# A fused adaLN block: the order of its opening, the loads and the third weight group

## The chip, the cores and the metric

The kernel runs on one core of one Trainium2 chip. The metric is device time in microseconds (us). The engines of the core are called by the names of the profile: PE is TensorE (matrix products), DVE is VectorE, ACT is ScalarE, POOL is GpSimd, and SP is SyncE, which here only issues DMAs.

## The reference, cut to what matters

```python
mod = (silu(c) @ wmod).reshape(2, 6, 1, 512)      # sa, ca, ga, sb, cb, gb
h = layernorm(x) * (1 + ca) + sa                  # x: 2 x 4096 x 512, float32
xn = h / norm(h) * sqrt(512) * gamma
q, kv, a = split(xn @ W_qkva.T, 3)                # W_qkva: 1536 x 512
y = scan(y[t] = sigmoid(a[t]) * y[t-1] + kv[t])   # along the 4096 tokens
x = x + floor(ga) * (q * y)
h = layernorm(x) * (1 + cb) + sb
x = x + floor(gb) * fp4_ffn(h)                    # gate, up, down: 512 -> 1408 -> 512
```

`floor` keeps the sign and raises the magnitude to at least 0.25. `fp4_ffn` quantises activations and weights to FP4 in blocks of 16. The change lies wholly in the first half, ahead of the first scans.

## The kernel before

The 8192 tokens are cut into 64 tiles of 128 tokens, and into 16 blocks of 512. The first half runs 64 **slots**: slot `4*i + e` multiplies block `i` by group `e` of the q/kv/a weights (group `e` holds 128 output features of each of the three parts, taken in the order `PARTS = (2, 1, 0)`). A product is float16 in two pieces: each operand is split into a high part (rounded to float16) and a low part (the rest), and three of the four combinations are summed, so one slot is 36 matmuls of 128x512 (`mix`, L393). Slot 0 is cut into four quarters of 128 tokens, so it can begin when the first tile is there.

To get an input tile ready, the kernel loads it (`norm_load`), takes its moments on DVE (`norm_moments`, L153), the inverse deviation on POOL (`norm_stats`, L160 and L161), centres and scales (`norm_center`, L166), shifts (`norm_shift`, L172), squares on ACT (`norm_square`, L354), computes the gain by a power on POOL (`norm_gain`, L359 and L361), writes the high part on ACT (`norm_hi`, L367) and the low part on DVE (`norm_lo`, L372), and transposes both by a DMA from SP (L376).

A weight group is prepared in a similar way: three loads (`load_part`, L208), a product with gamma (`gamma_qkva`, L281, on POOL unless DVE is asked for), squares on ACT (`square_qkva`, L285), a power on POOL (`inverse_qkva`, L288 and L289), the high part on ACT or DVE (`hi_qkva`, L308 or L310), the low part on DVE (`lo_qkva`, L316) and a transposing DMA (L324). `gain_qkva` (L296, L299) computes the factor with which the gate is scaled.

High and low parts share four buffers (`new_hl`). The modulation rows are products on PE (`mod_spread`, `mod_rows`, `mod_columns`) that use two PSUM buffers of their own; `mod_store` (L262, L263) copies such a row on ACT and sends it to DRAM from POOL. The products of a slot use PSUM banks 0 to 2 or 3 to 5 in turn. They are read in the next slot by `gates` (ACT, L405), `scan` (DVE, L411) and `read_out` (DVE, L420), and with these reads the banks come free for the slot after.

The order of work on every engine is written out by hand: all five engines issue their instructions in the order of the program, and the function `start` (L642 and the lines after it) is the opening, ahead of slot 0. SP works through its DMAs in program order too, and waits at each until its source is ready. Slots follow in a loop: input tile `slot + 4` gets its high and low parts, tile `slot + 5` is centred, shifted and squared, tile `slot + 6` gets its moments.

In the kernel before, groups 0 and 1 are prepared in `start`; group 2 is multiplied and squared in slot 0 and split in slot 1; group 3 is multiplied and squared in slot 1 and split in slot 2.

Of the kernel before, what the change touches and what calls it, by code (L numbers as in the profile page):

```python
# [17 lines left out]
P = 128  # L18
D = 512
KC = D // P  # L20
# [23 lines left out]
def tile_adaln_block(  # L44
# [147 lines left out]
    wm = {}  # L192
# [14 lines left out]
    def load_part(e, part):  # L207
        S.dma_start(wq[e, part], w_qkva[part * D + e * P : part * D + (e + 1) * P, :])  # L208

    def load_mod(s, pieces=1):  # L210
        w = KC // pieces
        for k in range(0, KC, w):
            S.dma_start(
                wm[s][:, k : k + w, :],
                wmod[k * P : (k + w) * P, s * D : (s + 1) * D].rearrange("(k p) e -> p k e", p=P),
            )
# [63 lines left out]
    def gamma_qkva(e, part, engine=G):  # L280
        engine.tensor_tensor(wq[e, part], wq[e, part], gam, ALU.mult)  # L281
# [5 lines left out]
    def inverse_qkva(e, a=0, b=3):  # L287
        V.tensor_scalar(rs[:, e, a:b], us[:, e, a:b], 1e-36, 2.0**-28, ALU.max, ALU.mult)  # L288
        G.tensor_tensor(rs[:, e, a:b], rs[:, e, a:b], mhalf[:, : b - a], ALU.pow)  # L289
# [40 lines left out]
    def norm_load(g):  # L330
        i, t = divmod(g, KC)
        if i not in xrows:
            xrows[i] = apool.tile([P, KC, D], F32, name="xr", tag="xr", bufs=4)
        xld[g] = xrows[i][:, t, :]
        b, t0 = divmod(g * P, N)
        S.dma_start(xld[g], x[b, t0 : t0 + P, :])

    def norm_moments(g):
        xstat[g] = moments(xld[g])

    def norm_stats(g):
        xstat[g] = mean_rstd(xstat[g])

    def norm_center(g):
        xh[g] = center(xld.pop(g), xstat[g][0], ca[g * P // N])
# [294 lines left out]
    sa = [ctile([P, D], F32, "sa0", tag="mod_s0"), None]  # L640

    def start():  # L642
        load_mod(1, KC)
        norm_load(0)
        load_mod(0, 2)
        S.dma_start(gam, gamma.partition_broadcast(P))
        for part in PARTS:
            load_part(0, part)
        for g in range(1, KC):
            norm_load(g)  # L650
        for part in PARTS:
            load_part(1, part)
        load_mod(2)
        pc = mod_spread(1, 0)
        ps = mod_spread(0, 0)
        r1 = mod_rows(1)
        r0 = mod_rows(0)

        norm_moments(0)
        norm_stats(0)  # L660
        A.activation(ca[0], pc, AF.Copy, bias=1.0)
        a, b_, c_ = PARTS
        gamma_qkva(0, a, V)
        square_qkva(0, a)
        gamma_qkva(0, b_, V)
        square_qkva(0, b_)
        inverse_qkva(0, a, a + 1)
        gamma_qkva(0, c_, V)
        inverse_qkva(0, b_, b_ + 1)
        norm_center(0)  # L670
        hi_qkva(0, a, True)
        square_qkva(0, c_)
        norm_moments(1)
        hi_qkva(0, b_, True)
        inverse_qkva(0, c_, c_ + 1)
        lo_qkva(0, a)
        norm_stats(1)
        A.copy(sa[0], ps)
        lo_qkva(0, b_)
        hi_qkva(0, c_, True)  # L680
        norm_shift(0)
        norm_square(0)
        norm_center(1)
        lo_qkva(0, c_)
        norm_gain(0, G)
        norm_shift(1)
        norm_hi(0)
        norm_square(1)
        norm_moments(2)
        norm_stats(2)  # L690
        norm_lo(0, xT)
        norm_gain(1, G)
        norm_hi(1)
        norm_center(2)
        norm_moments(3)
        norm_lo(1, xT)
        norm_load(KC)
        norm_shift(2)
        norm_square(2)
        norm_stats(3)  # L700
        norm_center(3)
        norm_gain(2, G)
        norm_hi(2)
        norm_shift(3)
        norm_square(3)
        norm_lo(2, xT)
        norm_gain(3, G)
        gamma_qkva(1, a, V)
        norm_hi(3)
        mod_store(*r1, tag="yh")  # L710
        mod_store(*r0)
        square_qkva(1, a)
        gamma_qkva(1, b_, V)
        norm_lo(3, xT)
        norm_load(KC + 1)
        load_qkva(2)
        inverse_qkva(1, a, a + 1)
        gamma_qkva(1, c_, V)
        square_qkva(1, b_)
        square_qkva(1, c_)  # L720
        norm_moments(KC)
        hi_qkva(1, a, False)
        inverse_qkva(1, b_, b_ + 1)
        norm_stats(KC)
        lo_qkva(1, a)
        inverse_qkva(1, c_, c_ + 1)
        hi_qkva(1, b_, True)
        hi_qkva(1, c_, True)
        norm_center(KC)
        lo_qkva(1, b_)  # L730
        norm_shift(KC)
        norm_square(KC)
        lo_qkva(1, c_)
        norm_load(KC + 2)
        load_qkva(3)
        norm_gain(KC, G)
        gain_qkva(0)
        norm_moments(KC + 1)
        norm_stats(KC + 1)
        gain_qkva(1)  # L740

    units, coming = [], []
    gate = rows = None
# [5 lines left out]
    with order:  # L749
        xT = new_xT()  # L750
        start()
        for slot in range(NS + 3):
            i, e = divmod(slot, KC)
            if e == 0 and slot < NS:
                if slot:
                    xT = nxT
                nxT = new_xT() if i + 1 < NBLK else None
            units, coming = coming, load_units(plan[slot]) if slot < len(plan) else []
            g = slot + KC
            if g + 3 < NT:  # L760
                norm_load(g + 3)
            cur = mix(i, xT, e) if slot < NS else None
            late = rows
            rows = None
            if slot == 0:
                cols = mod_columns(2)
            elif slot in MODS:
                rows = mod_rows(MODS[slot])
            if 0 < slot < 3:
                for part in PARTS:  # L770
                    hi_qkva(slot + 1, part, False)
                    lo_qkva(slot + 1, part)
            if gate is not None:
                gate = gates(*gate)
            if len(joining) == 2 or slot >= NS + 2:
                residual(*joined(*joining.pop(0)))
            if g < NT:
                norm_hi(g)
            if slot < 2:
                for part in PARTS:  # L780
                    gamma_qkva(slot + 2, part)
                    square_qkva(slot + 2, part)
            if gate is not None:
                gate = scan(*gate)
            if slot == 1:
                signed_floor(gq, cols, atile([P, KC, B], F32, "mag"))
                prep_gain(0)
            if g + 2 < NT:
                norm_moments(g + 2)
            if gate is not None:  # L790
                gate = read_out(*gate)
            if g < NT:
                norm_lo(g, nxT)
            if gate is not None:
                joining.append(halves(*gate))
            if g + 2 < NT:
                norm_stats(g + 2)
            for u in units:
                u.advance(1)
            if g + 1 < NT:  # L800
                norm_center(g + 1)
            for u in units:
                u.advance(2)
                u.advance(3)
            if g + 1 < NT:
                norm_shift(g + 1)
                norm_square(g + 1)
            for u in units:
                u.advance(4)
            coming = [Unit(*c_) for c_ in coming]  # L810
            for u in coming:
                u.advance(0)
            if g + 1 < NT:
                norm_gain(g + 1, G)
            for u in units:
                u.advance(5)
                u.advance(6)
            assert all(u.step == 7 for u in units)
            if slot < 2:
                scale_qkva(slot + 2)  # L820
            if 0 < slot < KC:
                prep_gain(slot)
            if slot + 2 in MODS:
                load_mod(MODS[slot + 2])
            if late is not None:
                mod_store(*late)
            if slot == KC + 1:
                ca[1] = mod_load(1, 1, "mod_c1")
                sa[1] = mod_load(0, 1, "mod_s1")
            if slot == NS - 6:  # L830
                mods_for(0)
                gbs[0] = mod_load(5, 0, "mod_gb")
                x1s = {n: load_x1(n) for n in range(4)}
            if NS - 5 <= slot < NS - 1:
                n = slot - NS + 5
                xst[n] = stats_x(x1s[n])
                if n in (1, 2):
                    run(quant_x(n - 1, x1s.pop(n - 1), xst.pop(n - 1)))
            gate = cur
# [182 lines left out]
```

## Time and profile before

| | |
|---|---|
| median of 3 runs | 1954.62 us (1951.86 to 1954.72) |
| the profiled execution's own time | 1952.46 us |
| its span, first to last instruction | 1950.6 us |
| PE busy | 1909.8 us (98%) |
| DVE, ACT, POOL busy | 1603.2, 993.5, 423.3 us |
| granted PE clock, mean | 0.992 |

All times in the text are counted from the start of the span. A row of a timeline gives the start of a group of like instructions, their busy time, engine, source line, operation, what it writes and reads, how many there are, and in brackets how long the engine stood idle before and what ended that. L12 is line 12 of the kernel. A stretch row gives the busy time of PE, weight loads, DVE, ACT and POOL with the number of instructions, then the granted PE clock, the share of the DMA engines, and GB/s. The name given to the end of a wait is inferred, and where that engine had long been done it was another cause, often a DMA.

### The profile page before, as it was taken

To read this page: it belongs to the slowest core of one execution; us is meant where nothing else is said; L and a number is where in the kernel's file an instruction comes from. 1 tells how busy PE (TensorE), PEld (TensorE's weight loads), DVE (VectorE), ACT (ScalarE), POOL (GpSimd) and SP (SyncE) were. 2 spreads that over 40 slices of the span, in tenths; PEclk is the share of its full clock that TensorE was granted. 3 is DMA by queue.
4 is the path that set the end of the run, shared out by engine and by line. 5 is a ranking of instruction groups with operands and counts; after the bars stand their busy time and mean duration, and the time that the engine had idled before them with its cause. 6 is when DMAs were issued, how large, how long until landed. Compare 5 with 4: busy or idle time off the path is not lost.

```text
span 1950.6 us, 25677 instructions
## 1 busy us (share of the span) xinstructions
PE 1909.8 (98%) x9220; PEld 902.5 (46%) x9220; DVE 1603.2 (82%) x2670; ACT 993.5 (51%) x1705; POOL 423.3 (22%) x606
## 2 busy tenths in 40 slices
PE   7799999999999999999999999999999999999998
PEld 4244444444444444444444444444444444444443
DVE  4777789999858988888888888888888888888864
ACT  3444467777755544445444544544444444444532
POOL 4544456666530100000000010001001000000000
PEclk8899999999999999999999999999999999999999
DMA  7687779999843443433443344334433433433333
GB/s 218 150 236 190 178 164 210 201 203 201 180 122 63 77 79 63 79 78 63 69 82 68 63 78 89 63 66 87 72 63 77 79 63 63 83 73 63 64 65 51
DMA packets 482975, 206.39 MB, mean 106 GB/s; under 512 B 439526, under 2 KB 440806, under 8 KB 482848
## 3 DMA queue, kind: packets, MB, share of 16 engines
q1 hardware_dynamic: 468112, 170.98, 40.9%
q0 software_dynamic: 14736, 33.78, 10.1%
q8 instruction: 72, 1.18, 0.3%
q14 instruction: 55, 0.45, 0.1%
HBM read 62.85 MB, written 33.58 MB: 49 GB/s over the span
## 4 chain that ended last, share of the span: by engine, by line
PE 79%; issue 5%; DVE 1%; DMA 0%; POOL 0%; SPq 0%; ACT 0%; POOLq 0%; ACTq 0%; DVEq 0%
PE mm L857 44%; PE sd L904 21%; PE mm L393 14%; DMA xT<-hl 0%; POOL out_dram L927 0%; DVE ld L172 0%; DVE hl L372 0%; DVE ld L166 0%; DVE y L420 0%; DVE xn L106 0%; SPq L575 0%; DVE st L153 0%; SPq L267 0%; SPq L529 0%; DVE hl L129 0%
## 5 line engine op out<-in xcount | busy, mean ns | idle before, releaser
L857 PEld LDWEIGHTS <-x2T 128*128 128x128 f16 x4608 | 450.9, 98 | 469.4 <-issue 1.2
L393 PE MATMUL mm<-xT,wqT 128*128 128x512 f16 (+1 forms) x2412 | 510.2, 375 | 26.7 <-DMA xT<-hl 11.6
L857 PE MATMUL mm<-wuT,x2T 128*128 128x512 f16 (+1 forms) x2304 | 487.7, 361 | 1.0 <-DVE hid L877 1.0
L857 PE MATMUL mm<-wgT,x2T 128*128 128x512 f16 (+1 forms) x2304 | 487.7, 361 | 0.0
L904 PE MATMUL sd<-wdT,hT 128*128 128x512 f16 x2112 | 465.8, 379 | 0.0
L393 PEld LDWEIGHTS <-wqT 128*128 128x128 f16 x2412 | 234.1, 100 | 304.5 <-issue 29.4
L904 PEld LDWEIGHTS <-hT 128*128 128x128 f16 x2112 | 206.7, 98 | 242.6
L872 ACT ACTIVATE silu<-mm,u 128x512 f32<-128x512 f32 (+1 forms) x192 | 125.0, 652 | 285.9 <-PE mm L857 282.2
L877 DVE SCALAR_TENSOR_TENSOR hid<-mm,u,silu 128x512 f32<-128x512 f32 (+1 forms) x192 | 128.5, 673 | 139.6 <-PE mm L857 130.6
L587 POOL TENSOR_SCALAR rstd<-vs 128x1 f32<-128x1 f32 x64 | 14.1, 220 | 987.0 <-ACT sq L585 987.0
L143 ACT ACTIVATE u<-ud,rms 128x1 f32<-128x1 f32 x64 | 19.0, 297 | 277.7 <-DVE rms L139 277.7
L120 ACT ACTIVATE sle<-sl 128x512 f16<-128x512 f32 (+2 forms) x162 | 147.2, 909 | 0.0
L113 ACT ACTIVATE she<-sh 128x1408 bf16<-128x1408 bf16 (+1 forms) x128 | 128.5, 1004 | 4.1
L927 POOL DMA_DIRECT2D out_dram<-o x65 | 58.1, 898 | 275.8 <-DVE o L924 272.0
L411 DVE TENSOR_TENSOR_SCAN y<-sig,cy,mm 128x512 f32<-128x512 f32 x56 | 71.6, 1279 | 51.5 <-ACT sig L405 22.5
L122 DVE SCALAR_TENSOR_TENSOR xn<-hid,xn 128x1408 f32<-128x1408 f32 x64 | 103.6, 1619 | 3.7 <-ACT hid L116 3.7
L106 DVE TENSOR_TENSOR xn<-hid,inv 128x1408 f32<-128x1408 f32 x64 | 104.0, 1625 | 2.2
L125 DVE SCALAR_TENSOR_TENSOR hhl<-hid,xn 128x1408 f16<-128x1408 f32 x64 | 104.0, 1625 | 2.2
L147 DVE TENSOR_REDUCE amh<-hid 128x88 f32<-128x1408 f32 x64 | 103.7, 1620 | 2.2
L427 ACT COPY yh<-y 128x1024 uint16<-128x1024 uint16 x64 | 67.0, 1047 | 75.4 <-DVE y L420 75.4
L116 ACT ACTIVATE hid<-xn 128x1408 f32<-128x1408 f32 x64 | 88.3, 1379 | 30.7 <-DVE xn L106 30.7
L443 POOL TENSOR_TENSOR xr<-xr,y 128x512 f32<-128x512 f32 x64 | 81.4, 1271 | 55.1 <-ACT y L435 53.7
(113 smaller groups left out, 1920.4 us busy)
## 6 DMA issues: line engine op xcount, KB each, us to landing
xr<-in_L_attn_x_dram SPq DMA_DIRECT2D x64, 256.0 KB, 3.3
out_dram<-xr POOLq DMA_DIRECT2D x64, 256.0 KB, 3.7
ld<-out_dram SPq DMA_DIRECT2D x64, 256.0 KB, 2.9
out_dram<-o POOLq DMA_DIRECT2D x63, 256.0 KB, 3.9
ld<-in_L_ffn_w_gate_dram SPq DMA_DIRECT2D x22, 256.0 KB, 3.2
ld<-in_L_ffn_w_up_dram SPq DMA_DIRECT2D x22, 256.0 KB, 3.2
scratch<-in_L_wmod_dram SPq DMA_DIRECT2D x4, 1024.0 KB, 5.5
ld<-in_L_ffn_w_down_dram SPq DMA_DIRECT2D x16, 256.0 KB, 3.2
```

Of the source, the lines that this page charges most:

```text
L106: V.tensor_tensor(blocks(xn), blocks(src), spread(inv, nb), ALU.mult)
L113: A.activation(blocks(she), spread(sh, nb), AF.Copy, scale=WPEAK)
L116: A.activation(a, xn, AF.Abs, scale=MAGIC)
L120: A.activation(blocks(sle), spread(sl, nb), AF.Copy, scale=WPEAK)
L122: V.scalar_tensor_tensor(out=xn, in0=a, scalar=FLOOR, in1=xn, op0=ALU.max, op1=ALU.add)
L125: V.scalar_tensor_tensor(out=nq, in0=a, scalar=FLOOR, in1=xn, op0=ALU.max, op1=ALU.subtract)
L147: V.tensor_reduce(am, src.rearrange("p (b k) -> p b k", k=QB), AX.X, ALU.max, apply_absolute_value=True)
L393: T.matmul(pp[:, t : t + width], wqT[:, wp * KC + k, r * P : (r + 1) * P], xT[:, xp * KC + k, t : t + width], start=n == 0, stop=n == 3 * ...
L857: T.matmul(pp[:, : n1 - n0], x2T[:, xp * KC + k, :], wt[:, wp * KC + k, n0:n1], start=n == 0, stop=n == 3 * KC - 1,)
L872: A.activation(sl[:, :w], pairs[j][0][:, :w], AF.Silu, scale=u[:, 0:1])
L877: V.scalar_tensor_tensor(out=hid[:, n0:n1], in0=pairs[j][1][:, : n1 - n0], scalar=u[:, 1:2], in1=sl[:, : n1 - n0], op0=ALU.mult, op1=ALU.mult,
L904: T.matmul(pd, hT[:, hp * IC + k, :], wdT[:, wd_chunk(wp, k), :], start=n == 0, stop=n == 3 * IC - 1,)
```

## The change

Three things move. Weight 0 of the modulation is loaded in four pieces, and the parts of group 0 and input tile 1 are loaded between them. The order of the norm tiles' steps in `start` is rearranged; among other things the squares of tiles 0 and 1, and of tiles 2 and 3, stand ahead of the high parts of the first of each pair. And group 2 is prepared wholly inside `start`, so that group 3 is multiplied and squared in slot 0 and split in slot 1, behind that slot's read-out. The loads of group 1 and of modulation weight 2 (`load_mod(2)`, 1 MB) go from the beginning to places between the transposing DMAs.

```diff
     def start():
+        a, b_, c_ = PARTS
+
+        def load_mod_piece(s, k):
+            S.dma_start(wm[s][:, k, :], wmod[k * P : (k + 1) * P, s * D : (s + 1) * D])
+
         load_mod(1, KC)
         norm_load(0)
-        load_mod(0, 2)
         S.dma_start(gam, gamma.partition_broadcast(P))
-        for part in PARTS:
-            load_part(0, part)
-        for g in range(1, KC):
-            norm_load(g)
-        for part in PARTS:
-            load_part(1, part)
-        load_mod(2)
+        for k, then in enumerate((PARTS[0], PARTS[1], PARTS[2], None)):
+            if then is None:
+                norm_load(1)
+            else:
+                load_part(0, then)
+            load_mod_piece(0, k)
+        norm_load(2)
+        norm_load(3)
         pc = mod_spread(1, 0)
         ps = mod_spread(0, 0)
         r1 = mod_rows(1)
...
         norm_moments(0)
         norm_stats(0)
+        gamma_qkva(0, a, V)
         A.activation(ca[0], pc, AF.Copy, bias=1.0)
-        a, b_, c_ = PARTS
-        gamma_qkva(0, a, V)
         square_qkva(0, a)
         gamma_qkva(0, b_, V)
         square_qkva(0, b_)
         inverse_qkva(0, a, a + 1)
+        norm_center(0)
         gamma_qkva(0, c_, V)
         inverse_qkva(0, b_, b_ + 1)
-        norm_center(0)
         hi_qkva(0, a, True)
         square_qkva(0, c_)
+        lo_qkva(0, a)
+        inverse_qkva(0, c_, c_ + 1)
+        hi_qkva(0, b_, True)
         norm_moments(1)
-        hi_qkva(0, b_, True)
-        inverse_qkva(0, c_, c_ + 1)
-        lo_qkva(0, a)
         norm_stats(1)
+        lo_qkva(0, b_)
         A.copy(sa[0], ps)
-        lo_qkva(0, b_)
+        norm_center(1)
         hi_qkva(0, c_, True)
         norm_shift(0)
         norm_square(0)
-        norm_center(1)
         lo_qkva(0, c_)
+        load_qkva(1)
         norm_gain(0, G)
         norm_shift(1)
+        norm_square(1)
         norm_hi(0)
-        norm_square(1)
         norm_moments(2)
+        norm_moments(3)
+        norm_gain(1, G)
         norm_stats(2)
+        norm_hi(1)
+        norm_stats(3)
         norm_lo(0, xT)
-        norm_gain(1, G)
-        norm_hi(1)
+        load_mod(2)
         norm_center(2)
-        norm_moments(3)
-        norm_lo(1, xT)
-        norm_load(KC)
         norm_shift(2)
         norm_square(2)
-        norm_stats(3)
+        norm_lo(1, xT)
+        load_qkva(2)
+        norm_gain(2, G)
         norm_center(3)
-        norm_gain(2, G)
-        norm_hi(2)
         norm_shift(3)
         norm_square(3)
+        norm_gain(3, G)
+        norm_hi(2)
+        gamma_qkva(1, a, V)
         norm_lo(2, xT)
-        norm_gain(3, G)
-        gamma_qkva(1, a, V)
+        norm_load(KC)
         norm_hi(3)
-        mod_store(*r1, tag="yh")
-        mod_store(*r0)
+        gamma_qkva(1, b_, V)
         square_qkva(1, a)
-        gamma_qkva(1, b_, V)
+        square_qkva(1, b_)
         norm_lo(3, xT)
         norm_load(KC + 1)
-        load_qkva(2)
-        inverse_qkva(1, a, a + 1)
+        inverse_qkva(1, b_, a + 1)
         gamma_qkva(1, c_, V)
-        square_qkva(1, b_)
+        mod_store(*r1, tag="yh")
         square_qkva(1, c_)
+        mod_store(*r0)
+        hi_qkva(1, a, False)
+        inverse_qkva(1, c_, c_ + 1)
+        for part in PARTS:
+            gamma_qkva(2, part)
+        lo_qkva(1, a)
+        hi_qkva(1, b_, True)
         norm_moments(KC)
-        hi_qkva(1, a, False)
-        inverse_qkva(1, b_, b_ + 1)
+        hi_qkva(1, c_, True)
+        lo_qkva(1, b_)
         norm_stats(KC)
-        lo_qkva(1, a)
-        inverse_qkva(1, c_, c_ + 1)
-        hi_qkva(1, b_, True)
-        hi_qkva(1, c_, True)
-        norm_center(KC)
-        lo_qkva(1, b_)
-        norm_shift(KC)
-        norm_square(KC)
         lo_qkva(1, c_)
         norm_load(KC + 2)
         load_qkva(3)
+        norm_center(KC)
+        for part in PARTS:
+            square_qkva(2, part)
+        norm_shift(KC)
+        norm_square(KC)
         norm_gain(KC, G)
         gain_qkva(0)
         norm_moments(KC + 1)
+        inverse_qkva(2)
         norm_stats(KC + 1)
+        for part in PARTS:
+            hi_qkva(2, part, False)
+            lo_qkva(2, part)
         gain_qkva(1)
+        gain_qkva(2)
...
-            if 0 < slot < 3:
-                for part in PARTS:
-                    hi_qkva(slot + 1, part, False)
-                    lo_qkva(slot + 1, part)
...
-            if slot < 2:
+            if slot == 0:
                 for part in PARTS:
-                    gamma_qkva(slot + 2, part)
-                    square_qkva(slot + 2, part)
+                    gamma_qkva(3, part)
+                    square_qkva(3, part)
...
             if gate is not None:
                 joining.append(halves(*gate))
+            if slot == 1:
+                for part in PARTS:
+                    hi_qkva(3, part, False)
+                    lo_qkva(3, part)
...
-            if slot < 2:
-                scale_qkva(slot + 2)
+            if slot == 0:
+                scale_qkva(3)
```

## The prediction

> **What bounds the kernel now.** I read the page first (engine totals), then TensorE in order of time, then VectorE, GpSimd and the DMA share over the same stretch. "Slot" is the kernel's loop step; T is a transposing DMA.
>
> ```profile
> PE 1909.8 (98%) x9220; PEld 902.5 (46%) x9220; DVE 1603.2 (82%) x2670; ACT 993.5 (51%) x1705; POOL 423.3 (22%) x606
> ```
>
> TensorE is idle for 1950.6 - 1909.8 = 40.8 us. Where:
>
> ```profile
> 26.94 6.93 PE L393 MATMUL mm<-xT,wqT 128*128 128x128 f16 x72 [4.25 <-DMA xT<-hl]
> ...
> 40.41 4.59 PE L240 MATMUL sd<-sc,scratch 128*128 128x2 f32 x32
> 44.86 10.36 PE L393 MATMUL mm<-xT,wqT 128*128 128x512 f16 x36
> 58.51 2.76 PE L393 MATMUL mm<-xT,wqT 128*128 128x512 f16 x12 [3.29 <-DMA wqT<-hl]
> 62.17 5.34 PE L393 MATMUL mm<-xT,wqT 128*128 128x512 f16 x24 [0.89 <-DVE y L411]
> 73.44 9.74 PE L393 MATMUL mm<-xT,wqT 128*128 128x512 f16 x36 [5.93 <-DMA wqT<-hl]
> 86.83 40.70 PE L393 MATMUL mm<-xT,wqT 128*128 128x512 f16 x180 [3.66 <-ACT cy L414]
> ```
>
> Rows 3 to 7 are slots 1, 2 (two rows), 3 and 4 to 8. By 86.83 TensorE has idled about 24 us; from there it runs. Slots 2 and 3 wait for weight groups 2 and 3. Slot 4 waits, despite the name shown, for the T of tile 7: issued 82.22, landed 4.5 later. What feeds these waits is VectorE's chain:
>
> ```profile
> 13.94 1.33 DVE L281 TENSOR_TENSOR scratch<-scratch,gam 128x512 f32<-128x512 f32 x2 [3.74 <-DMA scratch<-in_L_attn_W_qkva_dram]
> ...
> 34.54 0.75 DVE L372 SCALAR_TENSOR_TENSOR hl<-ld,rn,hl 128x512 f16<-128x512 f32 x1 [1.21 <-ACT hl L367]
> ...
> 57.15 1.64 DVE L316 SCALAR_TENSOR_TENSOR hl<-scratch,rs,hl 128x512 f16<-128x512 f32 x1
> ...
> 60.90 1.21 DVE L411 TENSOR_TENSOR_SCAN y<-sig,mm 128x512 f32<-128x512 f32 x1
> ...
> 69.37 0.48 DVE L310 TENSOR_SCALAR hl<-scratch,rs 128x512 f16<-128x512 f32 x1 [2.12 <-POOL rs L289]
> ...
> 72.93 1.21 DVE L411 TENSOR_TENSOR_SCAN y<-sig,mm 128x512 f32<-128x512 f32 x1
> ...
> 78.98 1.22 DVE L411 TENSOR_TENSOR_SCAN y<-sig,mm 128x512 f32<-128x512 f32 x1 [1.16 <-ACT sig L405]
> ...
> 85.14 1.22 DVE L411 TENSOR_TENSOR_SCAN y<-sig,mm 128x512 f32<-128x512 f32 x1 [1.21 <-ACT sig L405]
> ```
>
> The scans of tiles e=0 to 3 mark slots 1 to 4: 60.90, then 12.03 later, then about 6.1 per slot. So the opening is bound by the VectorE-ScalarE-GpSimd chain, and the question is when the first scan starts.
>
> ```profile
> 45.95 3.71 POOL L281 TENSOR_TENSOR scratch<-scratch,gam 128x512 f32<-128x512 f32 x3
> ...
> 55.19 4.72 POOL L281 TENSOR_TENSOR scratch<-scratch,gam 128x512 f32<-128x512 f32 x3
> ```
>
> Three gamma products take GpSimd 3.71 with VectorE mostly idle, 4.72 beside VectorE, whose L316 then takes 1.64 instead of about 0.74.
>
> [...] Here a T lands 2.7 after issue alone, 5.2 right behind three 256 KB loads.
>
> **The change, part by part.**
>
> *Loads.* Before, gamma and the three parts of group 0 were issued behind 1 MB of modulation weight 0; landings: that weight 10.6 and 11.9, gamma 13.2, parts 13.8, 14.5, 15.4. Keeping that pace (0.65 per 256 KB, 1.3 for gamma) for the new order: part 1 at 11.3, part 2 at 12.6, part 3 at 13.9, weight 0's last piece at 15.8. So the first product starts at 11.3, not 13.94: -2.6. The price: the shift row (ScalarE, 18.48 before) waits for the last piece and two 0.43 matmuls, about 17.1; it still comes earlier, and the third high part, queued behind it on ScalarE, starts at 17.7 (19.25 before).
>
> *Norm tiles.* VectorE stalled 0.61 + 0.78 + 1.53 + 1.21 = 4.1 between 25.4 and 34.5, waiting for ScalarE's high parts behind GpSimd's powers. In the new order squares, moments and statistics fill these. From the third low part (ends 19.05) I add rows: shift 0.67, two moments 1.26, two aggregates 0.2, so 21.2; tile 0's high part (shift ends 18.35, square 0.8, GpSimd pair 1.3, high 0.72) is ready at 21.4; then low, center, shift, low, center, shift, one gamma product, low, product, low at 0.67 each plus one 0.9 wait for tile 2: the last low part ends at 29.0, before 35.2: -6.2.
>
> *DMAs moved.* Group 1's loads go behind group 0's Ts (20.3, landing about 24.4; used 25.5). Weight 2 (1 MB) moves from 14.56 to 23.6, ahead of tile 1's T; at 400 GB/s, 2.6 us, it lands about 28 and its use is near 37. Group 2's loads go ahead of tile 2's T. So Ts of tiles 1 to 3 land at about 29, 32 and 34, input tile 4 at 33. Slot 0 on TensorE then ends at 37 to 38, the column products (4.59) at 42, slot 1, cold, at 52.3 at the latest. The gate that frees slot 2's bank comes at 54.1, so all this hides; the cover is 1.8, and beyond it each us is one on slot 2. Of the four high/low buffers, group 1's third needs tile 2's T landed (32) and is taken at 33.6: no wait, but close. On SP the Ts of group 2, waiting for VectorE until 46.7, stand ahead of input tile 7's load and tile 4's T, needed at 56 and in slot 4.
>
> *Group 1 and group 2.* From 29.0: product 0.67 at 29.75, row copy and square to 31.4, second row copy and store to 32.7, power to 33.5. GpSimd then multiplies group 2, not shown in this place: 3.71 to 4.72 by the two rows above; 5.7 if each product waits out a VectorE instruction (3 x (0.65 + 1.24)); I take 4.3: 37.8. Queued behind these are tile 4's statistics 1.0, then shift 0.75, square 0.8, gain pair 0.9, two powers 1.7, hand-offs 0.2: 43.15. VectorE's high and low parts of group 2, 3 x 1.19 = 3.57: 46.7. Two powers 1.9: 48.6. Group 3's products (slot 0), again 3.71 to 4.72, taken 4.1: 52.7. Last square, tile 5's square, gate: 0.05 + 0.76 + 0.63 + 0.70: first scan at 54.8, before 60.90: -6.1. Group 2's Ts land by 49.8: slot 2 no longer waits for them but for bank 0, freed by the gate at 54.1.
>
> *Slot 1.* It gains group 3's high and low parts (3.57, nothing on GpSimd beside them) and loses the wait for the power and the stretched group 2. Rows: scan to read-out 2.91, to low 0.65, to its end 0.65, parts 3.57, aggregate and center 0.85, shift to gate 2.2: 10.8 instead of 12.03: -1.2. Slots 2 and 3 keep their period. Tile 7's T is issued at about 74.9, lands at 79.4 with the same 4.5, and slot 4 starts there instead of 86.83.
>
> Sum: -6.1 - 1.2 = -7.3. After slot 4 the instructions are those of before; scans at 94.00 and 101.77 wait for TensorE and the rest follows one or the other, so all shifts. The profiled execution's 1952.46 becomes 1945.2; it stands 2.2 below the median 1954.62, from which I forecast 1947.3.
>
> **Rivals.** (1) [...] both triples take 5.7: +1.4 + 1.6, gain 4.3, 1950.3. For it: the 1.64 row. Against: bn_stats and small operations lie between. (2) *The loads do nothing:* [...] gamma and part 1 still land at 13.9: gain 7.3 - 2.6 = 4.7, 1949.9. For: landings of 7.6 after issue. Against: they landed in issue order. (3) *Slower, the DMA queue:* weight 2, group 2 and Ts lie ahead of input tile 4, 2.62 MB from 25.2.
>
> ```profile
> 20.00:22.00 2.00, 2.00 (x6) 0.38 (x5) 2.00 (x4) 0.72 (x2) 1.50 (x3) 1.00 1.16 219
> 42.00:44.00 2.00, 2.00 (x15) 2.00 (x16) 1.44 (x5) 0.98 (x3) 1.47 (x3) 0.74 1.20 159
> ```
>
> The last column is GB/s: full engines moved only 159 to 219 with Ts among the loads. At 159, tile 4 lands at 41.7 and VectorE's moments, then lows, center, shift run from there: first scan about 60.3, gain 1.8 (1952.8). It decides from a landing of 43.5 on[...]. Against: loads alone ran at 404 (14 to 16 us), and no landing of a load here took over 8.0. (4) *More:* both triples near 3.71 (-1.0) and tile 7's T in 2.8 (-1.7): gain 10.0, 1944.6.
>
> **How the numbers follow.** Forecast 0.50; (1) 0.15; (2) 0.08; (3) 0.17, of which 0.10 slower by over 0.2%; (4) 0.10. A difference of 0.2%, 3.9 us, is about what a measurement can tell from none. Faster: 0.50 + 0.10 + two thirds of (1) and (2) = 0.75; slower 0.10; the rest 0.15. The forecast's own range is 1945 to 1950; with the others 1943.2 to 1953.8, leaving out the slower end of (3) and the far end of (4).
>
> **What would show it.** Right: first product near 11.3, last norm low part near 29, no VectorE wait for group 2's power after slot 0 began, scans near 54.8, 65.6, 71.7, 77.7, slot 4 near 79.4. Wrong: a wait of moments for input tile 4 beyond 36; GpSimd triples over 5; a scan-to-scan of slot 1 over 12; or TensorE's later gaps (near 255, 290, 541) growing by what the opening saved.

## The result, and the profile after

The kernel after the change takes 1948.74 us (median of 16 runs, 1945.48 to 1953.59) against 1953.03 for the kernel before on the same chip (16 runs, 1950.36 to 1955.7). The ratio is 0.9979, with an interval of 0.9972 to 0.9987: 4.1 us less, between 2.5 and 5.5. The sign was forecast, and the time lies 1.4 above the forecast 1947.3; the gain is a little over half of the 7.3 that was worked out. That the time came closer than the gain is luck: the forecast started from 1954.62, the median of three runs, which is 1.6 above the median of all 16.

The execution that was profiled took 1951.17 us, with a span of 1949.0: only 1.6 below the span before. The engine totals from the page:

```profile
PE 1912.0 (98%) x9220; PEld 901.3 (46%) x9220; DVE 1601.0 (82%) x2669; ACT 991.2 (51%) x1705; POOL 423.2 (22%) x605
```

TensorE has the same 9220 matmuls, yet was busy for 2.2 us longer. Part of the gain was lost inside the matmuls. TensorE in order of time (start, duration, group, and in brackets the idle time ahead of it):

```profile
26.23 2.17 PE L393 MATMUL mm<-xT,wqT 128*128 128x128 f16 x36 [2.65 <-DMA xT<-hl]
31.88 5.54 PE L393 MATMUL mm<-xT,wqT 128*128 128x128 f16 x72 [3.48 <-DMA xT<-hl]
...
40.13 3.69 PE L240 MATMUL sd<-sc,scratch 128*128 128x2 f32 x32
43.68 7.93 PE L393 MATMUL mm<-xT,wqT 128*128 128x512 f16 x36
56.30 18.72 PE L393 MATMUL mm<-xT,wqT 128*128 128x512 f16 x72 [4.69 <-ACT sig L405]
80.75 41.58 PE L393 MATMUL mm<-xT,wqT 128*128 128x512 f16 x180 [5.72 <-DMA xT<-hl]
...
251.95 32.93 PE L393 MATMUL mm<-xT,wqT 128*128 128x512 f16 x144 [2.18 <-ACT sig L405]
286.90 250.49 PE L393 MATMUL mm<-xT,wqT 128*128 128x512 f16 x1152 [2.02 <-DMA xT<-hl]
539.76 32.93 PE L393 MATMUL mm<-xT,wqT 128*128 128x512 f16 x144 [2.38 <-DMA xT<-hl]
```

Slots 2 and 3 are now one row of 72: neither waits for a weight group's T any more. Slot 4 starts at 80.75 instead of 86.83. The last three rows open later blocks; the kernel before has there:

```profile
257.27 32.94 PE L393 MATMUL mm<-xT,wqT 128*128 128x512 f16 x144 [2.29 <-DMA xT<-hl]
291.60 248.80 PE L393 MATMUL mm<-xT,wqT 128*128 128x512 f16 x1152 [1.40 <-ACT sig L405]
...
543.07 31.24 PE L393 MATMUL mm<-xT,wqT 128*128 128x512 f16 x144 [2.67 <-DMA xT<-hl]
```

So the lead is 6.1 at slot 4; slots 4 to 8 take 41.58 instead of 40.70, which leaves 5.2; it is 5.3 at slot 24, 4.7 at slot 28, 3.3 at slot 60, and 1.6 after the last row. In each of the last two steps the same matmuls take 1.69 longer than before (250.49 against 248.80, and 32.93 against 31.24); in the first of them a shorter gap ahead of slot 60 gives 0.3 back. VectorE, in the same view:

```profile
10.93 0.69 DVE L281 TENSOR_TENSOR scratch<-scratch,gam 128x512 f32<-128x512 f32 x1 [1.46 <-DMA scratch<-in_L_attn_W_qkva_dram]
...
28.83 0.75 DVE L372 SCALAR_TENSOR_TENSOR hl<-ld,rn,hl 128x512 f16<-128x512 f32 x1
...
36.89 0.69 DVE L153 BATCH_NORM_STATS2 st<-xr 128x6 f32<-128x512 f32 x1 [4.23 <-DMA xr<-in_L_attn_x_dram]
...
44.30 0.49 DVE L310 TENSOR_SCALAR hl<-scratch,rs 128x512 f16<-128x512 f32 x1 [2.58 <-POOL rs L289]
...
56.29 1.22 DVE L411 TENSOR_TENSOR_SCAN y<-sig,mm 128x512 f32<-128x512 f32 x1 [0.96 <-ACT sig L405]
...
67.08 1.22 DVE L411 TENSOR_TENSOR_SCAN y<-sig,mm 128x512 f32<-128x512 f32 x1 [1.16 <-PE mm L393]
```

The first gamma product and the last norm low part came within 0.6 us of the forecast. Then a new wait stands ahead of 36.89: for 4.23 us VectorE waits for input tile 4, whose moments come next. The prediction had named a wait for tile 4 beyond 36 as a sign of being wrong. The first scan starts at 56.29 (60.90 before), the second 10.79 later (12.03 before). GpSimd's two triples, each the three gamma products of one group:

```profile
33.49 3.72 POOL L281 TENSOR_TENSOR scratch<-scratch,gam 128x512 f32<-128x512 f32 x3
...
50.01 4.16 POOL L281 TENSOR_TENSOR scratch<-scratch,gam 128x512 f32<-128x512 f32 x3
```

Neither is near 5.

### The profile page after: what moved, and what is told of

The parts are those of the page before. It is cut to its first block, busy times and chain, and to the rows that moved or that the text cites. A ratio compares the mean times of both kernels' runs of the same rounds, so it can differ in the third digit from the quotient of the medians.

```text
span 1949.0 us, 25684 instructions
## 1 busy us (share of the span) xinstructions
PE 1912.0 (98%) x9220; PEld 901.3 (46%) x9220; DVE 1601.0 (82%) x2669; ACT 991.2 (51%) x1705; POOL 423.2 (22%) x605
## 4 chain that ended last, share of the span: by engine, by line
PE 79%; issue 5%; DVE 1%; DMA 1%; POOL 0%; SPq 0%; ACT 0%; POOLq 0%; ACTq 0%; DVEq 0%
PE mm L871 44%; PE sd L918 21%; PE mm L393 14%; DMA xT<-hl 1%; POOL out_dram L941 0%; DVE ld L172 0%; DVE y L420 0%; DVE hl L372 0%; DVE ld L166 0%; SPq L575 0%; DVE xn L106 0%; DVE st L153 0%; SPq L267 0%; SPq L529 0%; DVE hl L129 0%
```

## Experiments

Three questions were open: what each part gives alone, what tile 4's wait costs, and what the clock of TensorE does with the lead. Each ratio below is to the kernel before on the same chip: for the e runs on one chip (e1 to e4 beside a median of 1952.17 of 43 runs, e5 to e8 beside 1951.77 of 31), for the f runs on another (1952.82 of 15). So kernels are compared by their ratios; the changed kernel's is 0.9979.

### The loads alone (e1_loads)

```diff
-        load_mod(0, 2)
         S.dma_start(gam, ...)
-        for part in PARTS: load_part(0, part)
-        for g in range(1, KC): norm_load(g)
+        # parts 1, 2, 3 and norm_load(1), each ahead of a piece of weight 0
+        norm_load(2)
+        norm_load(3)
```

> The kernel before with the loads of weight 0 interleaved as in the change, and nothing else. Theory (the opening's chain sets the end): first product with gamma near 11 instead of 13.94, last norm low part about 2.5 earlier than 35.2, scans and slot 4 earlier by about 2.4 (first scan near 58.5, slot 4 near 84.4), time lower by about 2.4 us. Rival (the gain is lost on the way, to the shift row, which now comes from a later landing, or to the wait for input tile 6): first product earlier, first scan within 0.5 of 60.90, time unchanged.

Measured: 1950.17 us, ratio 0.9991 (0.9983 to 0.9999). VectorE in order of time:

```profile
45.84 0.69 DVE L153 BATCH_NORM_STATS2 st<-xr 128x6 f32<-128x512 f32 x1 [4.20 <-DMA xr<-in_L_attn_x_dram]
...
58.82 1.21 DVE L411 TENSOR_TENSOR_SCAN y<-sig,mm 128x512 f32<-128x512 f32 x1
```

The first scan is 2.1 earlier, most of the 2.6 that the first product gained. The loads do act; the rival that they do nothing falls. The ratio stands for 1.8 us less (0.2 to 3.3), where 2.4 were expected.

### Group 2 in the opening alone (e2_group2)

```diff
         inverse_qkva(1, c_, c_ + 1)
+        for part in PARTS: gamma_qkva(2, part)
...      # squares, powers, high and low parts of group 2 in the opening; group 3 in slots 0 and 1, as in the change
```

> The kernel before with group 2 prepared inside the opening and group 3 in slots 0 and 1, loads and norm order as before. Theory: first scan near 59.4 (group 2's products start near 41 instead of 45.95, the split no longer waits inside slot 1), scan to scan of slot 1 10.8 instead of 12.03, so slot 4 about 2.7 earlier, near 84.1, time lower by about 2.7 us. Rival (the work is only moved): first scan later by as much as slot 1 gets shorter, slot 4 within 0.5 of 86.83, time unchanged.

Measured: 1952.54 us, ratio 1.0004 (0.9996 to 1.0013). The first scan is where it was, the second 1.36 earlier:

```profile
60.78 1.22 DVE L411 TENSOR_TENSOR_SCAN y<-sig,mm 128x512 f32<-128x512 f32 x1 [0.96 <-ACT sig L405]
...
71.57 1.22 DVE L411 TENSOR_TENSOR_SCAN y<-sig,mm 128x512 f32<-128x512 f32 x1 [1.16 <-ACT sig L405]
```

So alone this part gives slot 1's 1.2 and nothing ahead of the first scan, and even the 1.2 cannot be found in the time: slot 4 waited 5.98 for its T, and slots 4 to 8 took 41.69. The first scan near 59.4 and the 2.7 us that were expected did not come.

### The order of the norm tiles alone (e3_norm)

```diff
-        norm_stats(1) ... norm_lo(3, xT)     # order of before
+        norm_stats(1) ... norm_lo(3, xT)     # order of the change, without its loads and group 2
```

> The kernel before with the norm tiles' steps and group 1's in the changed order; the loads and the place of group 2 as before. Theory: the 4.1 us of stalls between 25.4 and 34.5 go to about 1, last norm low part near 32 instead of 35.2, first scan near 57.6, slot 4 near 83.5, time lower by about 3.3 us. Rival (the wait of 5.30 for input tile 6 in slot 0, whose load stands behind group 1's transposes, takes the gain): first scan within 0.7 of 60.90, time lower by under 0.7.

Measured: 1950.67 us, ratio 0.9997 (0.9989 to 1.0005). The last norm low part starts at 31.79 (34.54 before), but:

```profile
46.84 0.70 DVE L153 BATCH_NORM_STATS2 st<-xr 128x6 f32<-128x512 f32 x1 [5.50 <-DMA xr<-in_L_attn_x_dram]
...
59.72 1.21 DVE L411 TENSOR_TENSOR_SCAN y<-sig,mm 128x512 f32<-128x512 f32 x1
```

Of 2.75 gained, 1.2 reach the first scan, where 3.3 were expected: as in the rival, VectorE waits for input tile 6, and longer. By the third scan the three parts alone give 2.1, 1.35 and 1.2, 4.65 in all; together they gave 5.85. What joins them, by these rows, is that wait: in the changed kernel group 2's high and low parts lie ahead of tile 6's moments, which then start at 48.00 without a wait.

### Tile 4's wait: earlier load (e4_x4), and the loads ahead of it (f1_mod2)

Both start from the changed kernel. The first moves one load, the second moves 1 MB out of the way.

```diff
# e4_x4
+        norm_load(KC)
         load_qkva(2)
...
         norm_lo(2, xT)
-        norm_load(KC)
# f1_mod2
         norm_load(3)
+        load_mod(2)
...
         norm_lo(0, xT)
-        load_mod(2)
```

> The changed kernel with input tile 4's load one place earlier, ahead of group 2's three loads. Theory (the wait of 4.23 at 32.7 to 36.9 for tile 4 is what put the first scan at 56.29 rather than 54.8): tile 4 lands near 33, the wait falls below 0.5, tile 4's statistics start right behind group 2's products near 37.3 instead of 38.42, first scan near 55.1, slot 4 near 79.6, time 1.2 us below the changed kernel. Rival: group 2's parts land later by one load, the products start later by 0.65 or more, and the first scan stays within 0.4 of 56.29.

> The changed kernel with modulation weight 2 (1 MB) loaded right behind input tile 3, where the queue is emptying, instead of ahead of tile 1's transpose. Theory (three things end within 1 us of each other near 37: tile 4's landing, GpSimd's three products[...], and tile 2's transpose, which frees a high/low buffer; one alone does not move the first scan): tile 4's moments wait under 1 instead of 4.23, a low part of group 1 takes over 3 beside GpSimd's products, first scan between 55.7 and 56.5. Rival (the late landing alone costs the 1.5 that the forecast missed): first scan at 55.0 or below.

Measured: 1947.54 us, 0.9979 (0.9971 to 0.9987), and 1948.62 us, 0.9974 (0.9963 to 0.9985). The first scans, at 56.10 and 56.19, hardly moved, although tile 4's moments now start at 32.84 and 34.50. What took the wait's place in the first, on VectorE:

```profile
33.45 4.60 DVE L316 SCALAR_TENSOR_TENSOR hl<-scratch,rs,hl 128x512 f16<-128x512 f32 x1
```

and on GpSimd:

```profile
33.77 3.72 POOL L281 TENSOR_TENSOR scratch<-scratch,gam 128x512 f32<-128x512 f32 x3
```

In the second, beside a triple of 3.73:

```profile
34.50 0.69 DVE L153 BATCH_NORM_STATS2 st<-xr 128x6 f32<-128x512 f32 x1 [1.49 <-DMA xr<-in_L_attn_x_dram]
35.11 3.03 DVE L316 SCALAR_TENSOR_TENSOR hl<-scratch,rs,hl 128x512 f16<-128x512 f32 x1
```

An instruction of 0.75 lasted 4.60 and 3.03, until about 0.55 after GpSimd's third product was done, and all of VectorE's work stood behind it. In the changed kernel VectorE had nothing to issue during the triple, because tile 4 was late. So two covers of nearly equal length lay over each other, the late tile and the blocked VectorE; taking one away gives about nothing. f1's expectation had foreseen this, but for tile 4's wait, which was 1.49 and not under 1. e4's had put the whole loss on the late tile, and that is refuted; nor did its rival's reason come true, for the triple began only 0.28 later than in the changed kernel.

### Both covers off (e5_vector, f2_vector_mod2)

e5 is e4 with groups 2 and 3's gamma products on VectorE, spread over tile 4's work; f2 also loads weight 2 early.

```diff
-        for part in PARTS: gamma_qkva(2, part)
+        gamma_qkva(2, a, V)
         norm_center(KC)
+        gamma_qkva(2, b_, V)
+        square_qkva(2, a)
         norm_shift(KC)
         norm_square(KC)
+        gamma_qkva(2, c_, V)
...
-                    gamma_qkva(3, part)
+                    gamma_qkva(3, part, V)
```

> The changed kernel with input tile 4 loaded ahead of group 2, and the gamma products of groups 2 and 3 on VectorE instead of GpSimd, group 2's spread between tile 4's center and shift. Theory (a low part of group 1 was blocked for the whole of GpSimd's three products, 4.60 in the run with only the load moved[...]): group 1's low parts take 0.75 again, no VectorE instruction over 1.2 before the first scan except scans, group 2's split starts near 41 instead of 44.3, first scan near 51 to 52, slot 4 near 76, time 4 to 5 us below the changed kernel. Rival (VectorE is the fuller engine, six products of 0.67 on it only move the bound): first scan within 1 of 56.1.

> As the run with the products of groups 2 and 3 on VectorE and tile 4's early load, with modulation weight 2 also loaded early. Theory (with all three gone the opening is bound by its own instructions): group 1's third high part no longer waits 3.08 for a transpose (under 0.8), first scan near 51.5 instead of 54.08, slot 4 near 75.7 instead of 78.28, time about 2.5 us below that run. Rival (the wait goes to something else, the column products or slot 1 on TensorE): first scan above 53.3.

Measured: 1945.02 us, 0.9966 (0.9953 to 0.9979), and 1944.24 us, 0.9955 (0.9943 to 0.9967). In e5 the first scan came at 54.08, 2.2 sooner than in the changed kernel, but not at the 51 to 52 expected. ScalarE shows why:

```profile
36.69 0.72 ACT L308 ACTIVATE hl<-scratch,rs 128x512 f16<-128x512 f32 x1 [3.08 <-DMA xT<-hl]
```

Group 1's third high part takes the buffer of tile 2, whose T had not landed: the buffer that the prediction called close. With weight 2 out of the way of that T, VectorE's wait for this part falls from 2.38 to 0.33. The first scan of f2, on VectorE:

```profile
51.44 1.22 DVE L411 TENSOR_TENSOR_SCAN y<-sig,mm 128x512 f32<-128x512 f32 x1 [1.14 <-ACT sig L405]
```

and its slot 4, on TensorE:

```profile
75.71 32.78 PE L393 MATMUL mm<-xT,wqT 128*128 128x512 f16 x144 [4.10 <-DMA xT<-hl]
```

51.44 and 75.71, as expected of it: 4.85 and 5.04 sooner than in the changed kernel. In time, e5 is some 2.5 us below the changed kernel and not the 4 to 5 expected; f2 is 4.7 below it. The 2 us between e5 and f2 lie within their intervals.

### The clock after a wait (e6_warm4, e7_warm_all, f4_warm24)

These are the changed kernel with matmuls whose sum nobody reads (fillers), issued while TensorE would wait: added work, nothing left out. A restart behind a gap is called cold where the clock is then half, and warm where it stays full.

```diff
+    def keep_warm(xT, n):
+        pm = side((P, TB))
+        for j in range(n):
+            T.matmul(pm, wqT[:, 0, :P], xT[:, 0, :], start=j == 0, stop=j == n - 1)
...
+            if slot in WARM: keep_warm(xT, WARM[slot])   # after the slot's own work
# e6: WARM = {3: 16}   e7: {3: 16, 23: 8, 27: 6, 59: 8}   f4: {3: 24}
```

> The changed kernel with 16 matmuls of 128x512 more, whose sum nobody reads, issued right behind slot 3's products, in the gap of 5.72 ahead of slot 4. Theory (the longer gap lets the TensorE clock fall, which costs slots 4 to 8 about 2.5: 41.58 us against 39.0 at full clock): gap about 2.3, slots 4 to 8 in 39.0, slot 4's start unchanged at about 80.7, time 2.5 us below the changed kernel. Rival (the stretch is a wait on banks or transposes, not the clock): slots 4 to 8 again in 41 to 42, time unchanged.

> As the run with 16 matmuls ahead of slot 4, and 8, 6 and 8 more ahead of slots 24, 28 and 60, in gaps of 2.0 to 2.4. Theory (each of these gaps costs 0 or 1.7 us by chance, four matmul slots in 31.2 or 32.9 us, and that is much of the spread of the runs): the slots behind the gaps run in 31.2, the spread of the runs falls below 5 us, time about 4 to 5 us below the changed kernel. Rival (the cold stretches come whatever fills the gap): rows of 32.9 remain, time as with slot 4 alone.

> The changed kernel with 24 filling matmuls ahead of slot 4 and nowhere else. Theory (a gap of about 2 sometimes still lets the clock fall: 39.02 behind 1.91 in one run, 41.0 behind 2.24 in another; a gap under 1 does not): gap under 1, slots 4 to 8 in 39.0, time 2 us below the changed kernel. Rival (where the gap falls in time decides, not its length): slots 4 to 8 above 40.

Measured: 1946.28 us, 0.9976 (0.9965 to 0.9988); 1947.03, 0.9977 (0.9971 to 0.9984); 1947.28, 0.9973 (0.9962 to 0.9984). Slot 4 in f4:

```profile
77.42 5.34 PE L406 MATMUL sd<-xT,wqT 128*128 128x512 f16 x24
82.60 39.02 PE L393 MATMUL mm<-xT,wqT 128*128 128x512 f16 x180
```

39.02 against 41.58: 2.56 us of slots 4 to 8 are the clock. Windows of 2 us show it, first in the changed kernel ahead of and in slot 4 (the third figure from the end is the granted clock, then DMA share and GB/s):

```profile
78.00:80.00 2.00, 0.00 (x0) 0.00 (x0) 0.79 (x2) 2.00 (x4) 1.03 (x3) 0.78 1.14 157
...
82.00:84.00 2.00, 2.00 (x6) 0.76 (x5) 1.88 (x4) 0.83 (x1) 1.84 (x3) 0.50 0.35 102
84.00:86.00 2.00, 2.00 (x6) 0.76 (x5) 0.00 (x0) 0.72 (x2) 1.14 (x3) 0.51 1.14 228
```

and then in f4:

```profile
84.00:86.00 2.00, 2.00 (x11) 0.87 (x9) 0.76 (x2) 1.11 (x3) 1.37 (x3) 1.00 0.94 213
```

Six matmuls in 2 us at half clock, eleven at full clock. But the totals did not follow: all three intervals overlap the changed kernel's, where 2 to 5 us less were expected, and e7's 21 runs spread over 6.1 us, not under 5. Two reasons are seen in the profiles. In f4 the fillers end at 82.76, about a microsecond after the T would have let slot 4 start (first scan 57.15 plus the changed kernel's 24.46 from scan to slot 4 is 81.61). And in e7 a gap of 2.24 was left, after which slots 4 to 8 still took 41.1, while in e6 1.91 left them at 39.02.

f4's rival, that it matters where a gap falls in time, can be tried on the profiles. The rows above give the moments at which the changed kernel's clock changed: 0.78 from 78 to 80 means that it fell to half at 79.1, and 0.51 from 84 to 86 that it came back just before 86. Windows of 0.25 us give 79.13 and 85.96, and further on 253.21, 256.63, 287.35, 290.77, 539.93 and 543.35. All of these lie on marks 3.413 us apart (from 79.13 to 539.93 are 135 steps). In the profile of the kernel before the clock changed at 25.91, 32.74, 42.98, 49.80, 70.28, 77.11, 87.35, 90.76, 258.02 and 261.43: again marks 3.413 apart (from 25.91 to 258.02 are 68 steps), 1.39 out of step with those of the changed kernel.

For the gaps in these two profiles, what counts is how much of one lies between two marks. There are eight ahead of slots 4, 24, 28 and 60. Behind the six that had 2.02 to 3.41 us between two marks the clock fell at the next mark: 2.89 of 3.66 and all of 2.29 (slots 4 and 24) in the kernel before; 3.41 of 5.72, 2.15 of 2.18, all of 2.02 and all of 2.38 in the changed one. Behind the other two, both in the kernel before, it did not: 1.40 (slot 28), and 2.67 (slot 60), which a mark cuts into 0.92 and 1.75. Ahead of slots 2 and 3 the kernel before fits as well: its gap of 3.29, cut into 1.41 and 1.88, was followed by full clock (1.00 from 58 to 60), and in its 5.93, with 2.77 ahead of the mark at 70.28, the clock fell there (0.50 from 72 to 74). e7's 2.24 lay whole between two marks: its windows of 2 us (0.81 from 82 to 84, 0.84 from 86 to 88) put the fall at about 83.24 and the return at 86.64. At these seven cold restarts the clock stayed half for one step or two; one step at half clock costs 1.7 us of work, which is the 1.69 seen above.

The length of a gap parts them less well. The 14 profiles have 50 gaps of 0.7 us or more ahead of these four slots. By the rows behind them (warm is within 0.4 of 39.02 for slots 4 to 8, and of 31.24, 248.80 and 31.24 for the others), all ten of at most 1.94 us were warm and all ten of at least 3.53 cold; of the 30 from 1.95 to 3.38, 16 were cold.

These three kernels have the changed kernel's opening, and also say how far tile 4's landing wanders from profile to profile. Its moments start at 37.88, 38.81 and 37.75 (36.89 in the changed kernel's own profile) and the first scans at 57.28, 58.21, 57.15 and 56.29: 19.40 later each time. In these four profiles the first scan follows tile 4's landing one for one; e4 and f1 show that this ends when it lands earlier.

### Together (e8_best, f3_all)

e8 is e5 with e7's fillers; f3 is f2 with 24, 8, 8 and 10.

```diff
# e8: e5 and WARM = {3: 16, 23: 8, 27: 6, 59: 8}
# f3: f2 and WARM = {3: 24, 23: 8, 27: 8, 59: 10}
```

> The products on VectorE and tile 4's early load, with the filling matmuls ahead of slots 4, 24, 28 and 60. If the two act in different places the gains add: 4 to 5 from the opening and 4 to 5 from the clock, time about 9 us below the changed kernel, near 1939. If filling only hides what a shorter opening saves, it stays within 2 us of the better of the two.

> As the run before it in this list, with 24, 8, 8 and 10 filling matmuls ahead of slots 4, 24, 28 and 60. Theory: the gap ahead of slot 4 falls below 1, slots 4 to 8 run in 39.0, the later blocks in 31.2, time about 3 us below the kernel without filling and about 12 below the kernel before, near 1940. Rival: the clock still falls, rows of 41 or 32.9 remain, time within 1.5 of the kernel without filling.

Measured: 1942.02 us, 0.9952 (0.9939 to 0.9965), and 1941.01 us, 0.994 (0.9928 to 0.9952). f3's TensorE:

```profile
72.90 5.34 PE L406 MATMUL sd<-xT,wqT 128*128 128x512 f16 x24
78.08 39.31 PE L393 MATMUL mm<-xT,wqT 128*128 128x512 f16 x180
...
246.99 31.24 PE L393 MATMUL mm<-xT,wqT 128*128 128x512 f16 x144 [0.43 <-issue]
...
281.12 249.12 PE L393 MATMUL mm<-xT,wqT 128*128 128x512 f16 x1152 [1.17 <-DMA xT<-hl]
...
532.92 31.24 PE L393 MATMUL mm<-xT,wqT 128*128 128x512 f16 x144 [0.52 <-DMA xT<-hl]
```

All four restarts are within 0.4 of the warm times (39.02, 31.24, 248.80, 31.24), and the five runs lie within 1.7 us (1940.87 to 1942.54), where other kernels' spread over 3 to 8, though mostly in more runs (f2's five over 3.4). f3 beats both kernels: 11.7 us below the one before, between 9.4 and 14.1. The buffer wait was back in its profile (1.77 on VectorE, first scan 52.93), so even it isn't at its end. The expectations of f3 came out (near 1940, 12 below the kernel before). e8 did not reach its 9 us below the changed kernel: by the ratios it is 5.3 below. Its gap of 1.95 ahead of slot 4 was still followed by 40.71, and the one restart in later blocks that was still cold was at slot 28 (250.49), behind a gap of 2.05.

## Why the prediction was right, and too large

**A reading to correct.** TensorE had idled not about 24 but 26.8 us by 86.83 in the kernel before (the sum of its gaps). Nothing in the forecast rests on it.

**Loads: right.** First product forecast 11.3, measured 10.93; of the 2.6 forecast for the loads, e1 shows 2.1 at the first scan.

**Norm order: right at its place.** Last norm low part forecast to end at 29.0, ended at 29.58. That it is worth so much only together with group 2, whose work covers tile 6's wait, the prediction did not say; e3 and e2 alone show 1.2 and, ahead of the first scan, nothing.

**DMAs moved: mis-sized, the first error.** Input tile 4 was forecast to land at 33, and landed at 36.9 here, 37.8 to 38.8 in three other runs. The T of tile 2 was put at 32; it was issued at 28.3 and landed at 34.7. I let each transfer keep a usual latency and let them overlap, though the rates in the prediction's own view of before, 159 to 219 GB/s with Ts among the loads, were at hand. They went only into rival (3), and that was too dark with 159: two windows of the changed kernel have 259 and 229.

```profile
24.00:26.00 2.00, 0.00 (x0) 0.00 (x0) 1.90 (x3) 0.72 (x2) 1.44 (x3) 1.00 1.15 259
...
34.00:36.00 2.00, 2.00 (x32) 2.00 (x31) 0.00 (x0) 1.21 (x3) 2.00 (x3) 0.81 1.80 229
```

The truth lay between the forecast and rival (3), whose wait behind the transfers ahead was at work (without the 1 MB ahead of tile 4, in f1, its moments began at 34.50 instead of 36.89), but whose landing of 41.7 and small gain did not come. The landing is not the whole of it: in e4 tile 4 was there at 32.84, as forecast, and the first scan still came at 56.10. The forecast had no term for a VectorE instruction that waits out GpSimd's products (4.60 in e4).

**The chain from group 1 to the first scan.** The power of group 1's third part ended at 33.53 (33.5), the triple at 37.21 (37.8). Tile 4's statistics ended at 40.05 instead of 38.8: they began 0.6 late, behind the moments, and took 1.63 instead of 1.0. The split of group 2 began 1.15 late at 44.30 and took its 3.56; two powers and their hand-off cost 2.2 instead of 1.9; group 3's triple 4.16 (4.1). First scan 56.29 instead of 54.8: the term "-6.1" was -4.6 in this profile. Over the four profiles of kernels that share this opening, the mean first scan is 57.23, a gain of 3.7 against the one profile of before. That the kernel before has such a scatter too can't be excluded, with one profile of it.

**Rival (1), both triples at 5.7: a third thing happened.** The first triple was not stretched (3.72), and the second little (4.16). It was VectorE that stood still, for three GpSimd instructions in a row: 4.60 in e4, with GpSimd at its undisturbed 3.72; with the products moved to VectorE, in e5, the same instruction took 0.73. In the changed kernel that cost lay hidden beneath tile 4's wait of 4.23.

**Rival (4), half at most.** The first triple was short (3.72), the second 4.16, and tile 7's T took 4.3, not 2.8.

**Slot 1: right.** 10.79 from scan to scan, forecast 10.8; slots 2 and 3 kept their period.

**"So all shifts": the second error.** Slot 4 started at 80.75, and the gap before it grew from 3.66 to 5.72, because TensorE's slot 3 moved further (it ends at 75.02 instead of 83.18) than the T, which follows the scans. Around the restart the clock was half for longer (79.13 to 85.96, against 87.35 to 90.76): 0.9 us given back, where the prediction had TensorE's instructions cost what they did before. Then come the three restarts at the start of later blocks. Of 33 such restarts in the eleven profiles without fillers there, 16 were cold, most at 1.69, two at 2.6 and 2.8: 6, 4 and 6 of 11 by slot; as each of these slots was cold in some profiles and warm in others, that is chance in a single one. The changed kernel's profile had all three cold, before's had one. That is why the spans differ by only 1.6; without those two, 1.6 + 3.4 = 5.0. The prediction named growing gaps there as a sign of being wrong; the gaps hardly grew (2.18, 2.02, 2.38 against 2.29, 1.40, 2.67: 0.2 in sum), the matmuls behind them did.

The medians then fit: 3.7 at the first scan and 1.2 in slot 1 are 4.9, less the clock's 0.9 at slot 4 4.0, against 4.1 measured. This sum is an estimate: the first scan before is known from one profile, and e6 and f4 together did not resolve the clock's part in the total.

## What to carry to other kernels

When two waits lie over each other, look at what the second does when the first is gone: here a late tile and a blocked VectorE each hid the other, and only both removed gave 2 to 5 us. Cost a reordered opening by the bytes in flight ahead of each transfer rather than by the latency that a transfer had elsewhere (the T of tile 2 took 6.4 us to land here, where one alone had taken 2.7), and look at buffers called "close". And an earlier start of a matmul stretch is not all kept if the wait ahead of it grows (5.72 ahead of slot 4 instead of 3.66, and 41.58 behind it instead of 40.70): compare the same matmuls' durations in both profiles, and do not read a difference of two spans where restarts are cold by chance. Ahead of slots 4, 24, 28 and 60, the ten gaps of 0.7 to 1.94 us were all followed by full clock, by the times of the rows behind them.

## What the runs showed that was not expected

- The length of a gap alone does not decide the clock. Ahead of slot 4 gaps of 1.95 (e8) and 2.24 (e7) were followed by 40.71 and 41.1 for slots 4 to 8, while gaps of 2.74 (e1) and 3.12 (e3) were followed by 39.02 and 39.01. Gaps of 3.66 to 5.98 there were always followed by 40.6 to 41.8. In the kernel before and the changed one the part of a gap between two marks went with the clock, at least 2.02 against at most 1.88; this is shown for these two profiles and e7's alone, and whether the limit is sharp stays open.
- Fillers that left a gap of at most 1.42 us gave warm restarts at slots 24 and 60 (31.24 each time); at slot 28 a gap of 1.63 had 248.80 and one of 2.05 had 250.49.
- One VectorE instruction can wait out a whole train of GpSimd instructions (4.60 us for an instruction of 0.75 in e4), where beside the triple of 4.72 in the kernel before the longest VectorE instruction took 1.64. What decides between the two stays open.
- The same load, at the same place of the program, landed up to 1.9 us apart from profile to profile (36.89 to 38.81).
